# A two-layer spectral kernel: operand forms in the Newton square roots, and column groups in the forward DFT over w

## The chip, the cores and the metric

The kernel runs on one core of a Trainium2 chip. The metric is the device time in microseconds of one execution, and for several executions their median.

## The reference

The input x is a float32 array of 32 images, 32 channels, 128 rows (h) and 128 columns (w). There are two layers, and each adds its result to its input.

The first layer normalises x over groups of two channels and then takes a matrix square root of every 128x128 channel by five steps of a coupled Newton iteration (1024 matrices in all):

```
Y = A / |A|;  Z = I
for 5 steps:  T = 0.5 * (3 I - Z Y);  Y = Y T;  Z = T Z
x = x + Y * sqrt(|A|)
```

The second layer normalises again, takes the real part of a two-dimensional Fourier transform, and keeps 64 of 128 row frequencies (the first 32 and the last 32) and the first 32 column frequencies. For every kept frequency it multiplies the 32 channels by a 32x32 matrix of weights, takes the inverse transform, and adds its real part:

```
X = fftn(gn(x), axes=(2, 3)).real
top = einsum('bixy,ioxy->boxy', X[:, :, :32, :32], weights1)
bot = einsum('bixy,ioxy->boxy', X[:, :, -32:, :32], weights2)
x = x + ifftn(zero-padded(top, bot)).real
```

## The kernel before

Everything is float32. The work has three phases. The first goes over the images: normalisation, the square roots, and the forward transform of each image to the kept frequencies, which stay in SBUF in the tile `xs` (partition, row frequency within a group of 16, column frequency, image). The second multiplies by the weights and transposes the result into `ot`. The third takes the inverse transform for each image, adds it to the first layer's output, which the first phase left in HBM (`mid`), and writes the result.

In the first phase, `prep` loads an image into `xt` (h on partitions) in four transfers on SP's queue and works out the statistics, mostly on VectorE. `newton` handles four channels at once, a "group" of four 128x128 matrices in one [128, 512] tile. Every product of two such tiles is four TensorE matmuls into one PSUM bank (`products`), and every transpose four TensorE transposes against an identity (`transposed`). A bank is taken out of PSUM by ScalarE as a plain copy (`taken`) or by VectorE as 1.5 I - 0.5 ps (`three_less`). GpSimd (POOL) writes the normalised group. Five PSUM banks serve these products, two the forward transform (`ps_ax`), one the statistics.

The first product of the iteration is with the identity, so that it needs none. With P standing for the matrix that would turn A into Y, the kernel before keeps `p` and the transpose of A, `at`, and multiplies

```
            for _ in range(NSTEPS - 2):
                ty = taken(products(p, at), "ty", 5)
                yield
                tt = three_less(products(p, ty), "tt", 5)
                yield
                p = taken(products(tt, p), "p", 6)
                yield
```

TensorE computes the transpose of its first operand times the second, so in this form every product comes out as the next one needs it, and the only transpose in a group is that of A.

`post` sends the finished image to `mid`, takes its statistics, and then, for each four channels, normalises (`xn`, on POOL), and transforms over h with the data as stationary operand and 128 columns of the table moving (64 frequencies, cosine and sine; line 271). ScalarE copies the result into `u`, with channels innermost. Then comes the transform over w (line 281): for each of 16 row indices, two accumulating matmuls with a 128x128 block of `u` stationary and 32 columns of the table moving. The bank that results has frequency rows and channels on partitions, and VectorE copies it to `xs` (line 290).

The order of the first phase is set by hand: four lanes each run one group's generator, started three rounds apart, each advancing by one `yield` per round; after each round one step of `prep` or `post` (the list `back`) is taken. The tile framework then places the instructions on the engines' queues, keeping dependencies. [...]

Of the kernel before, what the change touches and what calls it, by code (L numbers as in the profile page):

```python
# [19 lines left out]
F32 = mybir.dt.float32  # L20
# [6 lines left out]
P = 128  # L27
B = 32
C = 32
# [3 lines left out]
EPS = 1e-5  # L33
KIN = 16
L = 32


T_FH = slice(0, 128)
T_FW = slice(128, 192)
T_IW = slice(192, 448)  # L40
T_IH = slice(448, 576)
T_COLS = 576


@with_exitstack
def conv_preact_kernel(
# [31 lines left out]
    with ExitStack() as phase:  # L78
# [90 lines left out]
        def bank(pool, tag):  # L169
            return pool.tile([P, 4, P], F32, tag=tag, name=tag)  # L170
# [26 lines left out]
        def newton(g, xt, nm, sc, sn):  # L197

            chans = range(4 * g, 4 * g + 4)
            a = nsp.tile([P, 4, P], F32, tag="a", name="a", bufs=4)
            for j, c in enumerate(chans):
                nc.gpsimd.tensor_scalar(  # L204
                    a[:, j, :],
                    xt[:, c, :],
                    nm[:, c // 2 : c // 2 + 1],
                    sc[:, c : c + 1],
                    ALU.add,
                    ALU.mult,  # L210
                )
            yield
            p = three_less(a, "p", 6)
            at = taken(transposed(a), "at", 5)
            yield
            for _ in range(NSTEPS - 2):
                ty = taken(products(p, at), "ty", 5)
                yield
                tt = three_less(products(p, ty), "tt", 5)
                yield  # L220
                p = taken(products(tt, p), "p", 6)
                yield
            ty = taken(products(p, at), "ty", 5)
            yield
            t = three_less(products(ty, p), "tt", 5)
            yield
            ps = products(ty, t)
            for j, c in enumerate(chans):
                nc.vector.scalar_tensor_tensor(  # L229
                    xt[:, c, :], ps[:, j, :], sn[:, c : c + 1], xt[:, c, :], ALU.mult, ALU.add  # L230
                )
            yield

        def post(b, xt):

            nc.sync.dma_start(out=mid[b], in_=xt)
            st = small.tile([P, C, 6], F32, tag="b_st", name=f"b_st{b}")
            for c in range(C):
                nc.vector.bn_stats(st[:, c, :], xt[:, c, :])
                if c % 8 == 7:  # L240
                    yield
            nm, pq = stats(st, "b")
            yield
            vg = small.tile([P, G], F32, tag="b_vg", name=f"b_vg{b}")
            nc.vector.tensor_reduce(
                vg, pq.rearrange("p (g c) -> p g c", c=2), AX.X, ALU.add
            )
            v = small.tile([P, G], F32, tag="b_v", name=f"b_v{b}")
            nc.vector.tensor_scalar(v, vg, 0.5, EPS, ALU.mult, ALU.add)
            s = root(v, G, "b_r", 256.0)  # L250
            r = small.tile([P, G], F32, tag="b_inv", name=f"b_inv{b}")
            nc.vector.reciprocal(r, s)  # L252
            yield

            u = up.tile([P, P, C], F32, tag="u", name=f"u{b}")
            for q in range(C // 4):
                xn = nsp.tile([P, 4, P], F32, tag="xn", name=f"xn{b}_{q}", bufs=2)
                for i in range(2):
                    g = 2 * q + i
                    nc.gpsimd.tensor_scalar(  # L260
                        xn[:, 2 * i : 2 * i + 2, :],
                        xt[:, 2 * g : 2 * g + 2, :],
                        nm[:, g : g + 1],
                        r[:, g : g + 1],
                        ALU.add,
                        ALU.mult,
                    )
                yield
                ps = bank(ps_ax, "ax")
                for j in range(4):  # L270
                    nc.tensor.matmul(  # L271
                        ps[:, j, :], xn[:, j, :], tab[:, T_FH], start=True, stop=True
                    )
                nc.scalar.copy(u[:, :, 4 * q : 4 * q + 4], ps.rearrange("w c m -> w m c"))
            yield

            uv = u.rearrange("w (s k r) c -> w s k (r c)", s=2, r=4)
            ps = ps_ax.tile([P, KIN, L], F32, tag="ax", name=f"f{b}")
            for kin in range(KIN):
                for s in range(2):  # L280
                    nc.tensor.matmul(  # L281
                        ps[:, kin, :],
                        uv[:, s, kin, :],
                        tab[:, T_FW.start + s * L : T_FW.start + (s + 1) * L],
                        start=(s == 0),
                        stop=(s == 1),
                    )
                if kin % 4 == 3:
                    yield
            nc.vector.tensor_copy(xs[:, :, :, b], ps)  # L290
            yield

        made = {}
# [32 lines left out]
    with ExitStack() as phase:  # L326
        wp = phase.enter_context(tc.tile_pool(name="wp", bufs=2))
        mp = phase.enter_context(tc.tile_pool(name="mp", bufs=2))
        ps_m = phase.enter_context(tc.tile_pool(name="ps_m", bufs=1, space=PSUM))
        ps_t = phase.enter_context(tc.tile_pool(name="ps_t", bufs=3, space=PSUM))  # L330
        for kq in range(4):
            wt = wp.tile([P, C, 4, L], F32, tag="wt", name=f"wt{kq}")
            for r in range(4):
                src = (w1, w2)[r // 2]
                k0 = (r % 2) * KIN + 4 * kq
                nc.sync.dma_start(
                    out=wt[32 * r : 32 * r + 32], in_=src[:, :, k0 : k0 + 4, :]
                )

            om = mp.tile([P, 4, 8, 4, L], F32, tag="om", name=f"om{kq}")  # L340
            for lh in range(2):

                pm = [
                    ps_m.tile([P, 16, C], F32, tag=f"pm{r}", name=f"pm{kq}_{lh}_{r}")
                    for r in range(4)
                ]
                for k4 in range(4):
                    for l in range(16):
                        for r in range(4):
                            nc.tensor.matmul(  # L350
                                pm[r][32 * k4 : 32 * k4 + 32, l, :],
                                xs[32 * r : 32 * r + 32, 4 * kq + k4, 16 * lh + l, :],
                                wt[32 * r : 32 * r + 32, :, k4, 16 * lh + l],
                                start=True,
                                stop=True,
                            )
                for r in range(4):
                    src = pm[r].rearrange("p l (o4 og) -> p og o4 l", o4=4)
                    dst = om[:, r, :, :, 16 * lh : 16 * lh + 16]
                    if r % 2:  # L360
                        nc.vector.tensor_copy(dst, src)  # L361
                    else:
                        nc.scalar.copy(dst, src)
            for r in range(4):
                omr = om[:, r].rearrange("p og o4 l -> p og (o4 l)")
                for h in range(2):
                    pt = ps_t.tile([P, 4, 4, B], F32, tag="pt", name=f"pt{kq}_{r}_{h}")
                    for i in range(4):
                        nc.tensor.transpose(pt[:, i].rearrange("p k b -> p (k b)"), omr[:, 4 * h + i, :], ident)  # L369
                    k0 = KIN * r + 4 * kq  # L370
                    dst = ot[:, 4 * h : 4 * h + 4, k0 : k0 + 4, :]
                    if h:
                        nc.vector.tensor_copy(dst, pt)
                    else:
                        nc.scalar.copy(dst, pt)
# [41 lines left out]
def _table():  # L417

    import numpy as np

    k = np.concatenate([np.arange(32), np.arange(96, 128)])
    n = np.arange(P)
    row = 2 * np.pi * (np.outer(n, k) % P) / P
    col = 2 * np.pi * (np.outer(n, np.arange(L)) % P) / P
    t = np.zeros((P, T_COLS))
    rows = np.stack([np.cos(row), np.sin(row)]).reshape(2, P, 4, KIN)
    t[:, T_FH] = rows.transpose(1, 0, 3, 2).reshape(P, P)
    t[:, T_IH] = rows.transpose(0, 2, 3, 1).reshape(P, P)
    t[:, T_FW] = np.concatenate([np.cos(col), -np.sin(col)], 1)
    t[:, T_IW] = np.tile(np.concatenate([np.cos(col).T, -np.sin(col).T], 1) / (P * P), (4, 1))  # L430
    return t.astype(np.float32)

# [22 lines left out]
```

## Time and profile before

| | |
|---|---|
| Time, median of 3 runs | 4153.58 us (4152.88 to 4153.66) |
| Profiled execution | time 4153.58 us, span 4151.8 us |
| TensorE matmul / weight load busy | 3973.8 us (96%) / 3781.8 us (91%) |
| VectorE, ScalarE, POOL busy | 1983.4 us (48%), 1498.5 us (36%), 730.4 us (18%) |
| First phase | to about 3400 us |
| Granted TensorE clock | 1.00 in most of the first phase, mean 0.954 |

Busy time is the union of an engine's instructions, and TensorE's matmuls and weight loads stand in rows of their own (PE and PEld), since a load can lie beside a matmul. A float32 product appears as two pairs of load and matmul, a transpose as one. A row of the page gives line, engine, operation, output and input tiles, shapes and count, then the busy time in us and the mean of one in ns, then the idle time of the engine just ahead of it with what ended it. The means of matmuls contain the way through the array, so that what a stream of them costs is read from the distance between starts.

### The profile page before, as it was taken

To read this page: it belongs to the slowest core of one execution; us is meant where nothing else is said; L and a number is where in the kernel's file an instruction comes from. 1 tells how busy PE (TensorE), PEld (TensorE's weight loads), DVE (VectorE), ACT (ScalarE), POOL (GpSimd) and SP (SyncE) were. 2 spreads that over 40 slices of the span, in tenths; PEclk is the share of its full clock that TensorE was granted. 3 is DMA by queue.
4 is the path that set the end of the run, shared out by engine and by line. 5 is a ranking of instruction groups with operands and counts; after the bars stand their busy time and mean duration, and the time that the engine had idled before them with its cause. 6 is when DMAs were issued, how large, how long until landed. Compare 5 with 4: busy or idle time off the path is not lost.

```text
span 4151.8 us, 90922 instructions
## 1 busy us (share of the span) xinstructions
PE 3973.8 (96%) x38784; PEld 3781.8 (91%) x38784; DVE 1983.4 (48%) x5766; ACT 1498.5 (36%) x2689; POOL 730.4 (18%) x1542
## 2 busy tenths in 40 slices
PE   7999999999999999999999999999999989987777
PEld 7999999999999999999999999999999988853333
DVE  5555555555555555555555555555555420023333
ACT  3444444444434444343344444334344320022222
POOL 2222222222222222222222222222222100000000
PEclk9999999999999999999999999999999975578998
DMA  2111111111111111111111111111111021168887
GB/s 65 42 42 42 42 42 42 42 42 42 42 42 42 42 42 42 42 42 42 42 42 42 42 41 39 37 40 40 40 39 38 21 62 22 22 203 280 285 285 247
DMA packets 291620, 282.95 MB, mean 68 GB/s; under 512 B 4368, under 2 KB 282896, under 8 KB 283024
## 3 DMA queue, kind: packets, MB, share of 16 engines
q1 hardware_dynamic: 159120, 210.02, 15.8%
q10 hardware_dynamic: 132096, 67.11, 5.5%
q8 instruction: 306, 5.01, 0.5%
q14 instruction: 98, 0.80, 0.1%
HBM read 142.90 MB, written 134.22 MB: 67 GB/s over the span
## 4 chain that ended last, share of the span: by engine, by line
PE 92%; DMA 2%; ACTq 2%; DVE 2%; ACT 1%; issue 0%; SPq 0%; POOL 0%; POOLq 0%; DVEq 0%
PE ns L186 65%; PE py L407 7%; PE pm L350 5%; PE ax L271 5%; PE f L281 5%; PE ns L194 3%; ACTq L411 2%; DMA xt<-in_x 2%; PE pg L396 1%; ACT gt L405 1%; PE pt L369 1%; DVE yt L409 1%; DVE a_st L136 0%; SPq L129 0%; DVE om L361 0%
## 5 line engine op out<-in xcount | busy, mean ns | idle before, releaser
L175 DVE SCALAR_TENSOR_TENSOR tt<-ns,eye 128x512 f32<-128x512 f32 x1024 | 704.8, 688 | 1111.3 <-PE ns L186 1104.8
L186 PE MATMUL ns<-at,p 128*128 128x128 f32 x8192 | 981.3, 276 | 1.4 <-DVE a_st L136 0.7
L186 PEld LDWEIGHTS ns<-at,p 128*128 128x128 f32 x8192 | 944.8, 192 | 2.1 <-ACT p L180 1.1
L180 ACT COPY p<-ns 128x512 f32<-128x512 f32 x768 | 449.7, 586 | 1062.2 <-PE ns L186 1058.1
L204 POOL TENSOR_SCALAR a<-xt,a_nm,a_sc 128x128 f32<-128x128 f32 x1024 | 444.3, 448 | 1789.0 <-PE ns L194 1423.2
L186 PE MATMUL ns<-p,tt 128*128 128x128 f32 x6144 | 754.5, 276 | 4.4 <-DVE tt L175 4.2
L186 PE MATMUL ns<-ty,p 128*128 128x128 f32 x6144 | 752.4, 276 | 0.4 <-ACT ty L180 0.4
L180 ACT COPY ty<-ns 128x512 f32<-128x512 f32 x1024 | 599.8, 586 | 403.2 <-PE ns L186 403.2
L186 PEld LDWEIGHTS ns<-p,tt 128*128 128x128 f32 x6144 | 719.4, 193 | 5.6 <-DVE tt L175 5.5
L186 PEld LDWEIGHTS ns<-ty,p 128*128 128x128 f32 x6144 | 717.8, 192 | 0.5 <-ACT ty L180 0.5
L260 POOL TENSOR_SCALAR xn<-xt,b_nm,b_inv 128x256 f32<-128x256 f32 x512 | 286.0, 569 | 865.8 <-DVE b_inv L252 467.0
L229 DVE SCALAR_TENSOR_TENSOR xt<-ns,a_t_s,xt 128x128 f32<-128x128 f32 x1024 | 288.4, 344 | 224.2 <-PE ns L186 224.2
L407 PE MATMUL py<-gt,tab 128*128 128x512 f32 x512 | 273.5, 683 | 115.2 <-ACT gt L405 112.6
L407 PEld LDWEIGHTS py<-gt,tab 128*128 128x128 f32 x512 | 105.8, 218 | 241.7 <-ACT gt L405 147.5
L409 DVE TENSOR_TENSOR yt<-py,yt 128x512 f32<-128x512 f32 x256 | 176.6, 692 | 297.9 <-PE py L407 289.4
L186 PE MATMUL ns<-p,ty 128*128 128x128 f32 x2048 | 280.5, 278 | 0.7 <-ACT ty L180 0.7
L271 PE MATMUL ax<-tab,xn 128*128 128x128 f32 x2048 | 272.1, 277 | 2.7 <-POOL xn L260 2.7
L186 PE MATMUL ns<-tt,ty 128*128 128x128 f32 x2048 | 273.2, 276 | 0.8 <-DVE tt L175 0.8
L405 ACT COPY gt<-pg 128x512 f32<-128x512 f32 x256 | 131.4, 599 | 341.1 <-issue 176.6
L271 PEld LDWEIGHTS ax<-tab,xn 128*128 128x128 f32 x2048 | 251.0, 193 | 3.2 <-POOL xn L260 3.0
L186 PEld LDWEIGHTS ns<-p,ty 128*128 128x128 f32 x2048 | 251.6, 192 | 0.9 <-ACT ty L180 0.9
L136 DVE BATCH_NORM_STATS2 a_st<-xt 128x6 f32<-128x128 f32 x1024 | 217.8, 279 | 68.0 <-DMA xt<-in_x 66.6
(75 smaller groups left out, 2795.8 us busy)
## 6 DMA issues: line engine op xcount, KB each, us to landing
xt<-in_x SPq DMA_DIRECT2D x128, 512.0 KB, 6.8
mid<-xt SPq DMA_DIRECT2D x32, 2048.0 KB, 6.3
yt<-mid SPq DMA_DIRECT2D x32, 2048.0 KB, 8.6
out<-yt ACTq DMA_DIRECT2D x64, 1024.0 KB, 8.0
wt<-in_L_conv_weights SPq DMA_DIRECT2D x16, 512.0 KB, 9.2
tab<-in_table SPq DMA_DIRECT2D x1, 288.0 KB, 3.0
```

What stands on the lines that cost most here:

```text
L136: nc.vector.bn_stats(st[:, c, :], xt[:, c, :])
L175: nc.vector.scalar_tensor_tensor(t, ps, -0.5, eye15, ALU.mult, ALU.add)
L180: nc.scalar.copy(t, ps)
L186: nc.tensor.matmul(ps[:, j, :], lhsT[:, j, :], rhs[:, j, :], start=True, stop=True)
L204: nc.gpsimd.tensor_scalar(a[:, j, :], xt[:, c, :], nm[:, c // 2 : c // 2 + 1], sc[:, c : c + 1], ALU.add, ALU.mult,)
L229: nc.vector.scalar_tensor_tensor(xt[:, c, :], ps[:, j, :], sn[:, c : c + 1], xt[:, c, :], ALU.mult, ALU.add)
L260: nc.gpsimd.tensor_scalar(xn[:, 2 * i : 2 * i + 2, :], xt[:, 2 * g : 2 * g + 2, :], nm[:, g : g + 1], r[:, g : g + 1], ALU.add, ALU.mult,)
L271: nc.tensor.matmul(ps[:, j, :], xn[:, j, :], tab[:, T_FH], start=True, stop=True)
L281: nc.tensor.matmul(ps[:, kin, :], uv[:, s, kin, :], tab[:, T_FW.start + s * L : T_FW.start + (s + 1) * L], start=(s == 0), stop=(s == 1),)
L350: nc.tensor.matmul(pm[r][32 * k4 : 32 * k4 + 32, l, :], xs[32 * r : 32 * r + 32, 4 * kq + k4, 16 * lh + l, :], wt[32 * r : 32 * r + 32, :, ...
L407: nc.tensor.matmul(py, tab[:, T_IH], gt, start=True, stop=True)
L409: nc.vector.tensor_add(xt[:, o : o + 4, :], py, xt[:, o : o + 4, :])
```

## The change

The change has two parts.

In `newton`, the iteration keeps `y` (Y) and `zt` (the transpose of Z). Each of the three inner steps computes T = 1.5 I - 0.5 Z Y, transposes T on TensorE, and multiplies for the new Y and the new Z's transpose. The first step has one product, the last two. The POOL output and Y share the tile tag `y` with eight buffers.

In `post`, the transform over h gives only the 65 columns that are different: 33 cosines (`KC`) and 32 sines (`KS`); cosines and sines of negative frequencies are the same up to a sign. The transform over w then has the table as stationary operand, 32 columns at a time, and `u` moving, up to 512 columns. Each of four frequency groups `r4` writes its own 32 PSUM partitions, so each occupies one 32-column group of TensorE, and two matmuls (cosine and sine) accumulate in each. The bank that results has column frequencies on partitions, and VectorE transposes it in 32x32 blocks on its way to `xs`, in place of the copy. The negative frequencies come in descending order, so the table for the inverse transform and the order of the weights' rows follow suit.

```diff
-T_FH = slice(0, 128)
-T_FW = slice(128, 192)
-T_IW = slice(192, 448)
-T_IH = slice(448, 576)
-T_COLS = 576
+KC = 33
+KS = 32
+T_FH = slice(0, KC + KS)
+T_FW = slice(65, 161)
+T_IW = slice(161, 417)
+T_IH = slice(417, 545)
+T_COLS = 545
...
             chans = range(4 * g, 4 * g + 4)
-            a = nsp.tile([P, 4, P], F32, tag="a", name="a", bufs=4)
+            y = nsp.tile([P, 4, P], F32, tag="y", name="y0")
             for j, c in enumerate(chans):
                 nc.gpsimd.tensor_scalar(
-                    a[:, j, :],
+                    y[:, j, :],
...
             yield
-            p = three_less(a, "p", 6)
-            at = taken(transposed(a), "at", 5)
+
+            zt = three_less(transposed(y), "zt", 8)
+            yield
+            y = taken(products(zt, y), "y", 8)
             yield
             for _ in range(NSTEPS - 2):
-                ty = taken(products(p, at), "ty", 5)
+                t = three_less(products(zt, y), "t", 5)
                 yield
-                tt = three_less(products(p, ty), "tt", 5)
+                tt = taken(transposed(t), "tt", 5)
                 yield
-                p = taken(products(tt, p), "p", 6)
+                py, pz = products(tt, y), products(t, zt)
+                y, zt = taken(py, "y", 8), taken(pz, "zt", 8)
                 yield
-            ty = taken(products(p, at), "ty", 5)
-            yield
-            t = three_less(products(ty, p), "tt", 5)
-            yield
-            ps = products(ty, t)
+            tt = three_less(products(y, zt), "tt", 5)
+            yield
+            ps = products(tt, y)
...
-            u = up.tile([P, P, C], F32, tag="u", name=f"u{b}")
+            u = up.tile([P, KC + KS, C], F32, tag="u", name=f"u{b}")
...
-                ps = bank(ps_ax, "ax")
+                ps = ps_ax.tile([P, 4, KC + KS], F32, tag="ax", name=f"h{b}_{q}")
...
-            uv = u.rearrange("w (s k r) c -> w s k (r c)", s=2, r=4)
-            ps = ps_ax.tile([P, KIN, L], F32, tag="ax", name=f"f{b}")
-            for kin in range(KIN):
-                for s in range(2):
+            ps = ps_ax.tile([P, KIN, C], F32, tag="ax", name=f"f{b}")
+            for s in range(2):
+                for r4 in range(4):
+                    first = (0, 16, 17, 1)[r4]
+                    skip = int(s == 1 and first == 0)
+                    at = first + skip if s == 0 else KC + first + skip - 1
+                    cols = T_FW.start + L * (0 if s == 0 else 1 + r4 // 2)
                     nc.tensor.matmul(
-                        ps[:, kin, :],
-                        uv[:, s, kin, :],
-                        tab[:, T_FW.start + s * L : T_FW.start + (s + 1) * L],
+                        ps[32 * r4 : 32 * r4 + 32, skip:, :],
+                        tab[:, cols : cols + L],
+                        u[:, at : at + KIN - skip, :],
                         start=(s == 0),
                         stop=(s == 1),
                     )
-                if kin % 4 == 3:
-                    yield
-            nc.vector.tensor_copy(xs[:, :, :, b], ps)
+            yield
+
+            nc.vector.transpose(xs[:, :, :, b], ps)
             yield
...
-                k0 = (r % 2) * KIN + 4 * kq
+                k0 = (4 * kq, KIN + 4 * kq, 12 - 4 * kq, 28 - 4 * kq)[r]
...
-                                wt[32 * r : 32 * r + 32, :, k4, 16 * lh + l],
+                                wt[32 * r : 32 * r + 32, :, (k4, 3 - k4)[r // 2], 16 * lh + l],
```

The host's table function follows: cosines and sines of 0 to 32 and 1 to 32 for the transform over h, the three blocks cosine, -sine, sine for w, and the rows of the inverse transform in the new order.

More of the change, by code (lines that the diff above doesn't have):

```diff
@@ L419, in _table @@
     import numpy as np
-    k = np.concatenate([np.arange(32), np.arange(96, 128)])
+    kin = np.arange(KIN)
+    k = np.concatenate([kin, KIN + kin, -(17 + kin), -(1 + kin)])
     n = np.arange(P)
-    row = 2 * np.pi * (np.outer(n, k) % P) / P
+    row = 2 * np.pi * (np.outer(k, n) % P) / P
+    mag = 2 * np.pi * (np.outer(n, np.arange(KC)) % P) / P
     col = 2 * np.pi * (np.outer(n, np.arange(L)) % P) / P
     t = np.zeros((P, T_COLS))
[L426 to L429, printed above, removed]
+    t[:, T_FH] = np.concatenate([np.cos(mag), np.sin(mag[:, 1:])], 1)
+    t[:, T_IH] = np.concatenate([np.cos(row), np.sin(row)])
+    t[:, T_FW] = np.concatenate([np.cos(col), -np.sin(col), np.sin(col)], 1)
     t[:, T_IW] = np.tile(np.concatenate([np.cos(col).T, -np.sin(col).T], 1) / (P * P), (4, 1))
```

## The prediction

> **What bounds the kernel now.** I read the page's busy shares first, then the busy time by stage, then the chain of work that ended last, and then TensorE's two rows in order of time.
>
> ```profile
> PE 3973.8 (96%) x38784; PEld 3781.8 (91%) x38784; DVE 1983.4 (48%) x5766; ACT 1498.5 (36%) x2689; POOL 730.4 (18%) x1542
> ```
>
> The table of three windows inside the first phase (columns: window; length; busy us and instructions of each engine; granted clock; DMA) says that this is no average over unlike stages: TensorE has no gap for 3 ms.
>
> ```profile
> 200.00:1200.00 1000.00, 998.59 (x8928) 998.26 (x8927) 534.42 (x1633) 400.36 (x714) 212.18 (x448) 1.00 0.13 41
> 1200.00:2200.00 1000.00, 998.65 (x8943) 998.32 (x8942) 531.30 (x1631) 401.00 (x715) 221.12 (x464) 1.00 0.13 41
> 2200.00:3200.00 1000.00, 998.90 (x8944) 998.57 (x8944) 533.27 (x1635) 403.74 (x721) 217.06 (x459) 1.00 0.13 41
> ```
>
> Some 8,930 matmuls in 1000 us are one each 112 ns, and so many weight loads. VectorE works 53% and ScalarE 40% of it. The chain of work repeats once per image; two of its longest pieces give the period, 1044.08 - 939.58 = 104.5 us.
>
> ```profile
> 939.58 9.01 PE ns L186 x80
> 1044.08 9.01 PE ns L186 x80
> ```
>
> An image issues, from the page's counts over 32: products 24576/32 = 768, transposes 1024/32 = 32, the DFT over h (L271) 64, the DFT over w (L281) 64, statistics 8: 936 pairs of load and matmul. 104.5 us / 936 = 111.6 ns. So the phase is a count of pairs, whatever their kind. The weight loads in order of time (start us, length us, then the instructions) show it for each kind:
>
> ```profile
> 2070.08 2.76 PEld L186 LDWEIGHTS ns<-ty,p 128*128 128x128 f32 x24
> 2072.76 1.87 PEld L281 LDWEIGHTS f<-tab,u 128*128 128x128 f32 x16
> ...
> 2077.81 0.47 PEld L194 LDWEIGHTS ns<-ident,a 128*128 128x128 f32 x4
> 2078.25 1.87 PEld L281 LDWEIGHTS f<-tab,u 128*128 128x128 f32 x16
> 2080.04 3.65 PEld L186 LDWEIGHTS ns<-at,p 128*128 128x128 f32 x32
> ```
>
> From start to start: products (2072.76 - 2070.08) / 24 = 112 ns; DFT over w, 32 moving columns, (2080.04 - 2078.25) / 16 = 112 ns; transposes (2078.25 - 2077.81) / 4 = 110 ns. A pair that moves 32 columns costs as much as one that moves 128: with 128x128 stationary, the load sets the pace. An f32 product is two such pairs (the page counts 8192 for 4 x 1024 products), a transpose one.
>
> **What the Trainium skill says.** "TensorE: Matmul & The Clock Gate", section "LDWEIGHTS (loading the stationary operand)", gives a load P/1.2 ns for P columns: 107 ns for 128. The trace agrees within 5% (111.6). The same page, "Part 3: Packing small matmuls — row/col tiling", says that matmuls on distinct 32-row or 32-column tiles run beside each other (2.38x for three column tiles). The trace has such a stage, the inverse DFT (32x64 tiles, four row and two column groups):
>
> ```profile
> 3707.52 0.19 PEld L407 LDWEIGHTS py<-gt,tab 128*128 128x128 f32 x1 [0.36 <-issue]
> 3707.95 0.19 PEld L407 LDWEIGHTS py<-gt,tab 128*128 128x128 f32 x1 [0.24 <-issue]
> 3708.38 0.19 PEld L407 LDWEIGHTS py<-gt,tab 128*128 128x128 f32 x1 [0.24 <-issue]
> ...
> 3709.33 1.40 PE L396 MATMUL pg<-tab,ot 32*64 32x128 f32 x64
> ```
>
> The first three lines, 0.43 us apart, price a pair of 512 moving columns at full array; 128 columns are a quarter, 0.107. The last line has 64 pairs of 128 columns in 1.40 us, not 64 x 0.107 = 6.9: 4.9 beside each other, more than four row groups alone give. "TensorEngine Tiling (Array Packing)", "Key Properties", says that changing the tiling mode drains TensorE; no line here isolates that.
>
> **The change, part by part** (against the profiled execution: span 4151.8, time 4153.58, which is also the median of the runs).
>
> *Square roots, products.* Before, a group of four channels takes 3 x 3 + 3 = 12 products and 1 transpose. After: 1 + 3 x (1 + 2) + 2 = 12 products and 1 + 3 = 4 transposes. Products add nothing. Three transposes of four channels in 256 groups are 3072 pairs; at the 0.110 us of above **+338 us**, all on the path, since TensorE has no gap to take them.
>
> *Square roots, evacuation.* ScalarE copies 8 banks a group before, 10 after: 512 x 0.586 = +300 us, less some 54 for the shorter copies of the DFT over h (below): from 40% to some 45% of the phase, hidden beside TensorE. VectorE keeps 5 banks a group (the first now from PSUM, 0.69 instead of 0.68). 0 us.
>
> *New waits.* A loop step is now t (VectorE), its transpose (ScalarE), then two products needing it. Lanes start three rounds apart and a group takes 15 rounds as before, so the four lanes stand at the same kind of step together: a round of transposes is 4 x 0.44 = 1.8 us of TensorE, where every round had up to 4 x 0.89 = 3.6. The last lane's transpose needs its t: VectorE 0.69 plus the 0.2 gap that the trace shows ahead of such reads; three transposes cover 1.3 us of it. The next round's first product needs ScalarE's 0.59 + 0.25, covered by 1.3. What gets in between is VectorE's other work ahead of t in its queue (four statistics, 0.86 us; four output adds, 1.13 us), and behind a blocked transpose stand all lanes. Bounds: 0, and 0.3 us in each of 256 x 15 / 4 / 3 = 320 such rounds, 96. Below nothing is excluded: there was no wait to remove. I take **+15**. PSUM stays at five banks for the products; each is held some 1.8 us of a group's 12.
>
> *POOL.* It writes y where it wrote a. a had four buffers of its own; y shares eight, five allocations a group. The buffer eight back is free at least one product round (5 us) earlier than needed, against 1.8 us of writing: 0, inside the bounds above.
>
> *DFT over h.* 65 moving columns for 128, same 2048 pairs with 128x128 stationary. By the L281 pace (32 columns, 112 ns) this saves **0**; bounds 0 and 8 us (down to 107). Its copy on ScalarE shrinks from 512 to 260 elements (at most half of 0.586 less; I take 0.21); hidden.
>
> *DFT over w.* Goes: 64 pairs an image, 7.14 us. Comes: 8 matmuls with 32 stationary columns and 512 (once 480) moving, 16 pairs, four column groups. Beside each other, each group does 4 pairs of 0.43 = 1.7 us; with the drain on both sides I take 2.1 (bounds 1.7 and 16 x 0.43 = 6.9, nothing overlapping). That is -5.0 x 31 = -156. The last image runs alone, 11.39 us at a granted clock of 0.62; after, some 3.8: -7.6. Together **-164**; bounds -176 and -8.
>
> *Block transpose.* VectorE's 32 copies at 1.053 us become transposes. "VectorE: DVE Perf Modes", "The three transpose paths", says it does 32x32 blocks only, which is what is wanted here; 311 ns for 128x128 bf16, by it an estimate of 4 x 311 = 1.2 us for 512 columns. Bounds 0.7 (a contiguous eviction) and 2.1; only the last image's stands on the path: 0 within 1 us. post has three steps fewer, so its tail is no longer.
>
> *The rest.* Weight loads from HBM keep count and size, each on SP as before; the mixing matmuls and inverse transforms only read other addresses; the table is 6% smaller. 0. Starting and draining four lanes with longer steps: +3.
>
> Sum: 338 + 15 - 164 + 3 = +192: 4153.6 + 192 = **4346 us**.
>
> **Rivals.**
>
> *Column groups do not run beside each other* (the change does not do what it says in its main part). The stationary is all 128 rows high here, and two column groups, never four, are seen sharing the array. Then the w-DFT is 6.9 us against 7.14: 338 + 15 + 3 - 8 = +348, 4502. Half overlap, each tile's second pass holding back the next tile, is 9 of 16 slots, 3.9 us: -100 instead of -164, 4410. Against: 4.9 beside each other in the inverse DFT.
>
> *The short round exposes latency.* 0.3 us in each of the 320 rounds: 4346 + 81 = 4427. For: all lanes are in step. Against: VectorE is half idle, and the trace shows statistics matmuls placed between a lane's products, so that TensorE's order leaves room to fill.
>
> *Faster: short matmuls are not paced by their weight load.* If a pair with few moving columns cost its stream (54 ns for a transpose's 128 columns in one pass, 55 for 65 columns in h), the transposes would add 166, the h-DFT would save 116 and the w-DFT 164: -114, 4040. It decides where the pace c meets 3072 c - 2048 (111.6 - c) = 164 us, c = 77 ns; below that the change is faster. Against it stand the L281 and L194 lines, both at 110 to 112.
>
> **How the numbers follow.** The likeliest case, four groups beside each other and few stalls, has 0.68, on its own 4310 to 4390; the exposed latency 0.14; half overlap 0.08, none 0.06; the fast case 0.02; the rest a lower granted clock (the page "TensorE: Matmul & The Clock Gate", "Part 4: PE-mode transpose", says that transposes do not count as activity; here the clock reads 1.00 through bursts of 0.44 us, and bursts become 1.8). The range 4295 to 4470 leaves out no overlap, the fast case and the tails, under 2 in 10. A difference of 0.2%, 8 us, is about what a measurement of this kernel can tell from no change; nearly all cases lie far above it: slower 0.97, same 0.01, faster 0.02.
>
> **What would show it.** Transposes 4096 on TensorE, still 110 ns apart; h-DFT pairs still 112 apart; the w-DFT some 2 us from first to last of 16; the image period near 110 us; TensorE still over 98% busy in the phase with waits for VectorE's t and ScalarE's tt of tens of us at most; ScalarE near 45% there; the stages after the first phase unchanged. Wrong would be: a period over 113, matmuls of a w-DFT starting 0.43 us apart, or transposes under 77 ns.

## The result and the profile after

| | before | after |
|---|---|---|
| Time, median of 4 | 4153.23 us (4150.50 to 4153.66) | 4348.14 us (4342.37 to 4352.01) |
| Profiled execution: time, span | 4153.58, 4151.8 us | 4352.01, 4350.2 us |
| First phase, to the first mixing matmul | 3399.7 us | 3591.3 us |
| Mixing phase | 268.8 us | 273.3 us |
| Inverse transforms | 483.3 us | 485.6 us |

The changed kernel is slower by 195 us: ratio 1.047, 95% interval 1.0451 to 1.0488. The forecast was 4346. In the profiled executions 191.6 us of it lie in the first phase. The 4.5 us in the mixing phase appear in some profiles of the changed kernel and not in others (269.4 in one of the experiments below), and nothing here explains them.

The busy times of the page of the changed kernel:

```profile
PE 4166.8 (96%) x40320; PEld 3900.9 (90%) x40320; DVE 1975.7 (45%) x5766; ACT 1726.6 (40%) x3201; POOL 720.3 (17%) x1542
```

TensorE has 40320 - 38784 = 1536 pairs more: 3072 transposes came, 1536 pairs of the DFT over w went. The count alone would be 1536 x 0.112 = 172 us.

The same three windows as before (length; busy us and instructions of PE, PEld, DVE, ACT, POOL; granted clock; DMA):

```profile
200.00:1200.00 1000.00, 997.92 (x8887) 977.52 (x8886) 501.42 (x1551) 445.11 (x823) 202.34 (x432) 1.00 0.12 40
1200.00:2200.00 1000.00, 999.09 (x8900) 977.75 (x8899) 503.84 (x1559) 443.51 (x821) 202.35 (x432) 1.00 0.12 40
2200.00:3200.00 1000.00, 999.05 (x8903) 979.20 (x8900) 503.10 (x1551) 445.66 (x825) 202.34 (x432) 1.00 0.12 39
```

TensorE's matmuls still fill the phase and ScalarE stands at 44 to 45%, as forecast. What differs is the weight-load row, 978 where it was 998: it now has gaps. From the groups by line and shape of the changed kernel (busy us, mean ns; idle ahead and its causes):

```profile
L196 PEld LDWEIGHTS ns<-ident,t 128*128 128x128 f32 x3072 | 346.1, 142 | 42.2 <-DVE t L177 18.6 <-DVE a_st L138 17.6 <-issue 0.8
L274 PE MATMUL h<-tab,xn 128*128 128x65 f32 x2048 | 262.9, 273 | 2.7 <-POOL xn L263 2.7
L277 ACT COPY u<-h 128x260 f32<-128x260 f32 x256 | 96.3, 376 | 296.2 <-PE h L274 296.2
L288 PEld LDWEIGHTS f<-u,tab 128*32 128x32 f32 x512 | 13.6, 110 | 24.2 <-issue 19.9 <-ACT u L277 0.7
L297 DVE STREAM_TRANSPOSE xs<-f 128x512 f32<-128x512 f32 x32 | 34.1, 1066 | 24.9 <-PE f L288 24.9
```

Some of these gaps belong to the new DFT over w: its 32-column loads are short (110 ns in the mean, against 192 for a product's), and the array streams meanwhile. Others are waits: the loads of the loop's transposes wait 36 us, for t or for statistics that stand ahead of t in VectorE's queue. The block transpose takes 1.066 us for the copy's 1.053.

TensorE in order of time around one DFT over w (start, length, instructions) shows both:

```profile
2083.75 1.00 PE L274 MATMUL h<-tab,xn 128*128 128x65 f32 x8
2084.59 2.90 PE L188 MATMUL ns<-y,zt 128*128 128x128 f32 x24
2087.42 1.92 PE L288 MATMUL f<-u,tab 128*32 128x512 f32 x16
2089.28 2.21 PE L196 MATMUL ns<-ident,t 128*128 128x128 f32 x12
2091.33 0.60 PE L196 MATMUL ns<-ident,y 128*128 128x128 f32 x4
...
2198.38 1.93 PE L288 MATMUL f<-u,tab 128*32 128x512 f32 x16
```

The 16 pairs of the DFT over w last 2089.28 - 2087.42 = 1.86 us; one after another at 0.43 they would need 6.9. The next comes after 110.96 us (the mean of 28 such periods in the trace is 110.6, against 104.5 in the part of the kernel before that the prediction showed). The round of transposes after it is the telling place: the 12 pairs of three lanes' t take 2.05 us where the last 4 take 0.43, the pace of 0.11. What holds them stands in the timeline of all engines for these microseconds:

```profile
2086.23 1.65 DVE L138 BATCH_NORM_STATS2 a_st<-xt 128x6 f32<-128x128 f32 x8 [0.88 <-DMA xt<-in_x]
2087.42 0.16 PEld L288 LDWEIGHTS f<-u,tab 128*32 128x32 f32 x8
...
2087.88 0.13 PEld L288 LDWEIGHTS f<-u,tab 128*32 128x32 f32 x4 [0.30 <-issue]
2088.30 0.13 PEld L288 LDWEIGHTS f<-u,tab 128*32 128x32 f32 x4 [0.30 <-issue]
2088.32 0.29 DVE L138 BATCH_NORM_STATS2 a_st<-xt 128x6 f32<-128x128 f32 x1 [0.44 <-DMA xt<-in_x]
2088.53 0.67 DVE L177 SCALAR_TENSOR_TENSOR t<-ns,eye 128x512 f32<-128x512 f32 x1
2089.12 0.28 DVE L138 BATCH_NORM_STATS2 a_st<-xt 128x6 f32<-128x128 f32 x1
2089.27 0.42 PEld L196 LDWEIGHTS ns<-ident,t 128*128 128x128 f32 x4 [0.84 <-DVE t L177]
...
2089.32 0.67 DVE L177 SCALAR_TENSOR_TENSOR t<-ns,eye 128x512 f32<-128x512 f32 x1
2089.91 0.28 DVE L138 BATCH_NORM_STATS2 a_st<-xt 128x6 f32<-128x128 f32 x1
2090.04 0.42 PEld L196 LDWEIGHTS ns<-ident,t 128*128 128x128 f32 x4 [0.35 <-DVE t L177]
```

VectorE works through the next image's statistics, waits for their load from HBM on the way, and only then makes t. TensorE's loads of transposes each wait for one t of 0.67 us. After the first 60 us, every wait of more than a few nanoseconds of these loads stands in this round, within 6 us of the start of the image's DFT over w; the other rounds of transposes run without one.

The lines also show the column groups at work: their loads come in sets of four, one for each group (the first two sets together), and each further set about 0.42 us after the last.

### The profile page after: what moved, and what is told of

Its sections match the earlier page's. It is cut to its first block, busy times and chain, and to the rows that moved or that the text cites. A ratio compares the mean times of both kernels' runs of the same rounds, so it can differ in the third digit from the quotient of the medians.

```text
span 4350.2 us, 94753 instructions
## 1 busy us (share of the span) xinstructions
PE 4166.8 (96%) x40320; PEld 3900.9 (90%) x40320; DVE 1975.7 (45%) x5766; ACT 1726.6 (40%) x3201; POOL 720.3 (17%) x1542
## 5 line engine op out<-in xcount | busy, mean ns | idle before, releaser
L188 PE MATMUL ns<-y,tt 128*128 128x128 f32 x8192 | 1087.7, 276 | 1.8 <-ACT tt L182 1.0
L188 PE MATMUL ns<-y,zt 128*128 128x128 f32 x8192 | 1024.9, 276 | 1.2 <-DVE zt L177 0.8
L188 PEld LDWEIGHTS ns<-y,tt 128*128 128x128 f32 x8192 | 994.6, 192 | 6.1 <-ACT tt L182 1.7
L188 PEld LDWEIGHTS ns<-y,zt 128*128 128x128 f32 x8192 | 965.0, 192 | 2.5 <-DVE zt L177 1.1
L177 DVE SCALAR_TENSOR_TENSOR t<-ns,eye 128x512 f32<-128x512 f32 x768 | 529.3, 689 | 663.1 <-PE ns L188 650.5
L188 PE MATMUL ns<-zt,t 128*128 128x128 f32 x6144 | 819.2, 275 | 0.0
L182 ACT COPY y<-ns 128x512 f32<-128x512 f32 x1024 | 600.4, 586 | 412.4 <-PE ns L188 412.4
L188 PEld LDWEIGHTS ns<-zt,t 128*128 128x128 f32 x6144 | 750.6, 192 | 0.0
L182 ACT COPY zt<-ns 128x512 f32<-128x512 f32 x768 | 450.2, 586 | 240.1 <-PE ns L188 240.1
L177 DVE SCALAR_TENSOR_TENSOR tt<-ns,eye 128x512 f32<-128x512 f32 x256 | 177.1, 692 | 701.5 <-PE ns L188 701.5
L196 PEld LDWEIGHTS ns<-ident,t 128*128 128x128 f32 x3072 | 346.1, 142 | 42.2 <-DVE t L177 18.6
```

Source lines behind the costliest of these rows:

```text
L177: nc.vector.scalar_tensor_tensor(t, ps, -0.5, eye15, ALU.mult, ALU.add)
L182: nc.scalar.copy(t, ps)
L188: nc.tensor.matmul(ps[:, j, :], lhsT[:, j, :], rhs[:, j, :], start=True, stop=True)
L196: nc.tensor.transpose(ps[:, j, :], t[:, j, :], ident)
```

## The experiments

Theory A, that of the prediction: the added transposes cost their pace on TensorE, column groups run beside each other, and a small rest is waits in the rounds of transposes. The rivals put the cost into the longer chain through VectorE and ScalarE, or deny the overlap of the column groups. The kernel before was run beside each set of experiments, and its median lay between 4152.92 and 4156.49 us; differences below some 5 us between kernels of different sets say nothing. Where starts of TensorE are added up below, each matmul counts with the distance from its start to the next one's start.

### Each part by itself

Only `newton` of the change (`post`, the tables and the mixing as before):

> Only the new form of the square roots, with the forward DFT of the kernel before. Theory A (the change costs its 3072 added transposes on TensorE, 0.110 us each, plus some 15 to 40 us of short waits): 4153 + 338 + 15 to 40 = 4506 to 4531 us. Theory B (TensorE has slack for the transposes, and the added time of the whole change comes from elsewhere): 4153 to 4250. If the two parts of the change add up, this run minus the changed kernel is what the new DFT gives, 160 to 180.

Measured: 4561.94 us (4555.51 to 4568.11), ratio 1.0977 (1.0958 to 1.0995), +405 us. That is above theory A's range by 31 us, and theory B is out.

Only the forward DFT of the change (`post`, the tables and the mixing as changed, `newton` as before):

> Only the new forward DFT (65 columns over h, column groups over w, block transpose), with the square roots of the kernel before. Theory A: four column groups run beside each other, so 64 pairs of 0.112 us become 1.9 us per image, with 0 to 13 us from the narrower DFT over h: 4153 - 164 to -185 = 3968 to 3989. If column groups gave only half overlap: 4050. If none: 4145. A change that does not interact: its difference to before plus that of the square roots alone makes the 195 us of both.

Measured: 3987.72 us (3985.91 to 3988.81), ratio 0.9594 (0.9579 to 0.9608), -169 us, inside the range of full overlap. This version beats both kernels.

The parts alone add up to 405 - 169 = 237 us; together they cost 195. So 42 us of the square roots alone are a matter of the company they keep. The trace of that kernel shows two things: its waits for t, 32 us, and a clock that falls. First its row in the view of waits (us in total, times, longest), then two windows of it (the granted clock is the third number from the end) and TensorE just before and in the first of them:

```profile
PEld ns L194 <- DVE t L175: 32.0, 64, 1.3
```

```profile
1026.00:1036.60 10.60, 10.60 (x54) 10.60 (x55) 1.12 (x4) 2.44 (x5) 0.00 (x0) 0.54 0.01 2
1036.66:1046.90 10.24, 10.24 (x94) 10.24 (x94) 2.81 (x5) 2.49 (x5) 1.75 (x4) 1.00 0.00 0
```

```profile
1018.70 2.84 PE L186 MATMUL ns<-y,zt 128*128 128x128 f32 x24
1021.38 1.87 PE L282 MATMUL f<-tab,u 128*128 128x32 f32 x16
1024.18 1.45 PE L194 MATMUL ns<-ident,t 128*128 128x128 f32 x8 [0.92 <-DVE t L175]
1025.95 1.12 PE L194 MATMUL ns<-ident,t 128*128 128x128 f32 x4 [0.33 <-DVE t L175]
1026.86 1.06 PE L194 MATMUL ns<-ident,y 128*128 128x128 f32 x4
1027.71 3.46 PE L282 MATMUL f<-tab,u 128*128 128x32 f32 x16
```

Full products run until 1021.4. Then come four microseconds of matmuls with 32 columns, a wait and transposes, and from 1025.5 on the same kinds of work run at half pace: 54 instructions in a stretch that otherwise holds 94. The trace has seven such stretches inside the phase, 58 us in all; half of that, some 29 us, is lost. The page "TensorE: Matmul & The Clock Gate" of the Trainium skill, "Part 4: PE-mode transpose", says that transposes do not count as activity for the clock. The falls here fit that, but do not isolate it. The kernel before has one such stretch too (713.9 us, 3.4 long), behind 32-column matmuls and a wait of 0.58 us, with no transpose in the six microseconds ahead; a kernel further below has one (1987.4 us, 3.4 long) behind transposes and a wait of 1.22 us, with no matmul of 32 moving columns. What all nine share is a DFT over w followed by a wait of TensorE of 0.3 to 1.2 us, within 5 us ahead of the fall. Other waits as long were followed by none (0.87 us at 2910.7 in this trace), so what it takes stays open.

The same kernel with its lanes four rounds apart:

```diff
-                if lanes[i] is None and todo and rounds >= 3 * i:
+                if lanes[i] is None and todo and rounds >= 4 * i:
```

> The new square roots with the forward DFT of before, lanes started four rounds apart. That form with lanes three apart took 4562, 68 more than 4156 + 338; its trace has 58 us at half clock inside the first phase and VectorE waits ahead of transposes. If both come from rounds in which four transposes stand together next to matmuls with 32 moving columns: 4494 to 4510, and no half clock in the phase. If the clock falls whatever the order of the lanes: above 4520.

Measured: 4482.04 us (4479.24 to 4484.86), +329 us, 12 below the range. The clock reads 1.00 in all three windows of its phase and the waits for t are 2 us. So both the half clock and the waits hang on the lanes standing at the same kind of step; since they go together, this run cannot say whether the clock fell for the transposes or for the waits. The two make some 59 of the 76 us that the other order of the lanes saves. Without them the square roots cost 329 / 3072 = 0.107 us a transpose. In the trace the transposes themselves start 111.7 ns apart, which is 343 us for the added ones; the other pairs start a little closer than in the kernel before (products 112.6 ns for 113.0, the DFT over w 108.7 for 112.0), which gives some 15 us back. Why is not known.

### Transposes or their chain

```diff
-                tt = taken(transposed(t), "tt", 5)
+                tt = taken(t, "tt", 5)
```

> The changed kernel without the transpose in the three inner steps: ScalarE copies t from SBUF where it copied the transposed t from PSUM, so the result is another matrix, while the order t, copy, two products and all waits on VectorE and ScalarE stay. 2304 groups' worth of nothing else changes; 3072 TensorE transposes go. Theory A (TensorE time): 4348 - 336 = 4012, less 10 to 30 if the short rounds of transposes exposed waits, 3982 to 4012. Theory B (the longer chain through VectorE and ScalarE costs the time): over 4250, since the chain is kept.

(The figure 2304 in that text is a slip; 3072 transposes go.) Measured: 4008.68 us (4005.45 to 4013.77), 339.5 us below the changed kernel, with the chain kept. So nearly all of the cost is TensorE's time for the transposes, and theory B is out.

The chain is not quite free, though. This kernel has exactly as many pairs as the one with the forward DFT alone (37248 on both pages), and is 21 us slower than its 3987.72. Its waits show where:

```profile
PEld ns L188 <- DVE tt L177: 19.7, 33, 1.0
```

The round of transposes has shrunk to the one of y, and the product behind it waits for VectorE's tt: the starts from a transpose to the next instruction take 133.9 us in the phase here, 114.2 with the forward DFT alone, for 1024 transposes each. So this run took some waits away with the transposes and put others in their place, and its 339.5 is the price of the transposes only because the two are about equal.

### The lanes' phases

The same edit, four rounds for three, in the changed kernel:

> The changed kernel with the lanes started four rounds apart in place of three, so that they no longer stand at the same kind of step together (15 rounds a group, steps repeat every 3). Theory A with waits in the short rounds: the rounds of four transposes go, and 15 to 30 us with them, 4318 to 4333. Theory C (the extra beyond the transposes is not due to the lanes being in step): within 5 us of the changed kernel's 4348.

Measured: 4327.30 us (4323.50 to 4329.05), 20.8 us below the changed kernel; its first phase ends at 3569.5 us, 21.8 earlier. The wait of the loop's transposes for t, in the view of waits (us in total, times, longest):

```profile
PEld ns L196 <- DVE t L177: 2.0, 3, 1.1
```

That row had 18.6 in the changed kernel, beside 17.6 for the statistics, which is gone. Of these 34 us, only 21 became time, since a load that waits while the array still streams the DFT over w delays nothing (shown under the next heading but one). So some 21 us of the change come from the lanes standing in step, most of it waits in the rounds of transposes: the starts from a transpose to the next instruction fall from 468.2 to 455.9 us, and those of the statistics' matmuls from 38.4 to 34.2.

### The column groups

The first group's sums done four times:

```diff
-            for s in range(2):
-                for r4 in range(4):
+            for s, r4 in [(s, 0) for _ in range(3) for s in range(2)] + [
+                (s, r4) for s in range(2) for r4 in range(4)
+            ]:
+                if True:
```

> The changed kernel, where the first column group works its own sums of the DFT over w four times over (three times ahead, overwritten by the last), the other three groups once: 28 pairs per image in place of 16, 12 of the added ones in one column group. Theory A (each column group streams at its own 0.43 us per 512 columns, beside the others): the first group's 16 pairs take 6.9 us where the stage took 1.86, so 5.0 us more per image, 4348 + 160 = 4508. Rival (no groups beside each other, a pair with few stationary columns just streams faster, 1.86 / 16 = 0.116 us each): 12 x 0.116 = 1.4 us more per image, 4393.

Measured: 4492.85 us (4491.76 to 4493.37), +144.7 us against the changed kernel, 4.5 an image, near the 5.0 of groups with a stream each and far from 1.4. TensorE in order of time:

```profile
2048.45 6.84 PE L290 MATMUL f<-u,tab 128*32 128x512 f32 x28
2055.22 1.53 PE L196 MATMUL ns<-ident,t 128*128 128x128 f32 x12
2056.59 0.60 PE L196 MATMUL ns<-ident,y 128*128 128x128 f32 x4
```

28 pairs take 6.77 us, just 16 x 0.42: the one long group, with the other three beside it. And the 12 pairs after it take 1.37 us where they took 2.05: the longer stage gives VectorE the time to make t. Over the phase the stage takes 155.5 us more, 4.9 an image, and the transposes 9.0 less, 0.3 an image. That is most of what the sum falls short of 5.0.

The loops exchanged, so that each group's matmuls are issued together:

```diff
-            for s in range(2):
-                for r4 in range(4):
+            for r4 in range(4):
+                for s in range(2):
```

> The changed kernel with the loops of the DFT over w exchanged: each column group's cosine and sine matmuls follow each other, and then comes the next group. Same 16 pairs. If TensorE lets a later column group start while an earlier one still has pairs waiting: 1.9 us per image as now, within 10 us of 4348. If a pair that waits for its own group holds up all behind it: 4 + 3 + 3 + 3 = 13 times 0.43 = 5.6 us, 3.7 more per image, 4348 + 118 = 4466.

Measured: 4351.44 us (4349.57 to 4357.49). No difference, and the stage takes 2088.10 - 2086.23 = 1.87 us:

```profile
2086.23 1.94 PE L288 MATMUL f<-u,tab 128*32 128x512 f32 x16
2088.10 1.77 PE L196 MATMUL ns<-ident,t 128*128 128x128 f32 x12
```

A later group starts while pairs of an earlier one still wait for their own columns.

### The width of the DFT over h

```diff
-                ps = ps_ax.tile([P, 4, KC + KS], F32, tag="ax", name=f"h{b}_{q}")
+                ps = ps_ax.tile([P, 4, P], F32, tag="ax", name=f"h{b}_{q}")
...
-                        ps[:, j, :], xn[:, j, :], tab[:, T_FH], start=True, stop=True
+                        ps[:, j, :], xn[:, j, :], tab[:, 0:P], start=True, stop=True
...
-                nc.scalar.copy(u[:, :, 4 * q : 4 * q + 4], ps.rearrange("w c m -> w m c"))
+                nc.scalar.copy(u[:, :, 4 * q : 4 * q + 4], ps[:, :, 0 : KC + KS].rearrange("w c m -> w m c"))
```

> The changed kernel with 128 moving columns in the DFT over h again (the 63 added columns are other parts of the table and their results are not used); copies and all else unchanged. Theory A (the weight load of 128 columns sets the pace): within 4 us of the changed kernel. Theory B (starts read 0.105 us apart with 65 columns in the changed kernel's trace, against 0.112: a real gain of 0.05 us per bank): 256 x 0.05 = 13 us slower, 4361.

Measured: 4373.03 us (4370.78 to 4377.77), 25 us slower: outside both theories. TensorE's pace is not the reason. The changed kernel, 65 columns:

```profile
2054.43 1.00 PE L274 MATMUL h<-tab,xn 128*128 128x65 f32 x8
2055.27 1.11 PE L188 MATMUL ns<-y,zt 128*128 128x128 f32 x8
2056.21 1.06 PE L188 MATMUL ns<-y,tt 128*128 128x128 f32 x8
```

This kernel, 128 columns:

```profile
2068.86 1.06 PE L274 MATMUL h<-tab,xn 128*128 128x128 f32 x8
2069.76 1.06 PE L188 MATMUL ns<-y,zt 128*128 128x128 f32 x8
2070.65 1.06 PE L188 MATMUL ns<-y,tt 128*128 128x128 f32 x8
```

With 65 columns the bank's eight pairs take 0.84 us to the next start and the following product 0.94; with 128 they take 0.90 and 0.89. Both sums are 1.78 or 1.79: the narrower matmul starts the product sooner and the product takes it back. It is so over the whole phase: the starts of the DFT over h take 222.9 us with 65 columns and 232.3 with 128, those of the products 2782.8 and 2773.4, and the two together 3005.7 in both kernels. What differs is the starts after the transposes and after the DFT over w, 13.6 and 8.6 us longer with 128 columns: waiting, by the view of waits of this kernel.

```profile
PEld ns L196 <- DVE t L177: 50.6, 71, 2.2
PEld ns L196 <- DVE a_st L138: 8.4, 10, 0.8
```

59 us for the 36 of the changed kernel. The instructions' order in the two kernels differs at this point: the framework put 29 of the next image's statistics ahead of the first t in VectorE's queue, where the changed kernel has 25 (both read from one image each). I took the late load of that image for the reason and gave it a fourth buffer, in both widths and in the kernel with the DFT alone:

```diff
-        xp = phase.enter_context(tc.tile_pool(name="xp", bufs=3))
+        xp = phase.enter_context(tc.tile_pool(name="xp", bufs=4))
```

> The changed kernel with four image buffers in place of three, so that the next image's load can start earlier. In the changed kernel the statistics of the next image stand ahead of t in VectorE's queue and wait for the load (84 us in all), and TensorE's transposes wait behind them, 36 us. If the late load is what makes the waits: 4348 less 15 to 30, 4318 to 4333. If it is the number of statistics in the queue and not their wait for the load: within 5 us of 4348.

Measured: 4347.70 us (4341.25 to 4351.73), no difference. In the profiled executions the waits for the load fell from 84 to 62 us and those of the transposes from 36 to 26, but these two executions are the slowest of the changed kernel's and the fastest of this one's, 11 us apart, while the medians agree.

> The changed kernel with 128 moving columns in the DFT over h and four image buffers. With three buffers the 128 columns cost 25 us, and VectorE's queue had 29 of the next image's statistics ahead of the first t in place of 25. If that cost is waits for the load in front of t: within 5 us of the kernel with 65 columns and four buffers. If it is the columns themselves: 13 to 25 us above that kernel.

Measured: 4365.47 us (4362.43 to 4373.03), 18 above the same kernel with 65 columns. The cost of the width stays, so the late load is not what makes it. The number lies where "the columns themselves" would put it, but the starts say otherwise again: the DFT over h and the products together take 3006.3 us in both kernels, and the starts after transposes 15.9 us more with 128 columns. So the cost is waiting for t. That the longer queue ahead of t makes the waiting is argued from the order and the waits: no kernel with the same order and the other width was run.

> The new forward DFT with the square roots of before and four image buffers. If the waits for VectorE's tt there come from the late load as well: 3965 to 3980, else 3988 within 5.

Measured: 3991.96 us (3991.12 to 3993.51): no gain.

> The new forward DFT with the square roots of before, lanes four rounds apart. With three apart it took 3988, and its trace has some 20 us in which TensorE waits for VectorE's tt after the short DFT over w. If those come from the lanes standing at the same kind of step: 3965 to 3980. If not: 3988 within 5.

Measured: 4007.91 us (4005.94 to 4012.20), 20 us slower than with lanes three apart. Both forecasts of a gain failed for one reason, in how I read the waits. The row of the kernel with the DFT alone was

```profile
PEld ns L188 <- DVE tt L177: 20.9, 25, 1.0
```

These waits come right after the DFT over w, while the array still streams its 512 columns. With the lanes four apart the load there waits for no tt, and yet the next product starts 0.52 us after the last matmul of the DFT over w in both kernels (the mean of 30 images). So a weight load that waits there delays nothing. Why the lanes four apart cost that kernel 20 us was not settled; 12 us of it lie in the starts of the products. The edit that helps one form of the square roots hurts the other, so the 21 us that it gained in the changed kernel may be net of such a loss.

## Why the prediction was right

**Bound.** The phase is a count of pairs. Over the whole phase a pair takes 113.0 ns in the kernel before and 112.4 with the square roots alone and lanes four apart, for the 111.6 of the prediction.

**Transposes, +338.** Taking them away gave 339.5, adding them alone without the waits 329. The term was right to 3%.

**DFT over w, -164.** 1.86 us for 2.1 assumed; the last image's is 3.19 for 3.8. The DFT alone gave -169. The rival of no overlap fell with the first group's quadruple work, that of half overlap with the 1.86 us and with the exchanged loops, which cost nothing.

**DFT over h, 0.** The size was right: what the narrower matmul saves, the products take back. The forecast that its pairs would still start 112 ns apart was wrong (0.84 us for eight, 105 ns). And the width is not free in the other direction: 128 columns would have cost 18 to 25 us more by way of waits for t. The prediction had no such term.

**Waits, +15.** Measured by the lanes' phases: 21, perhaps net. The place was the one forecast, a round of transposes with VectorE's statistics ahead of t, but the forecast had four statistics there and the trace has 25, which also wait for their load. The rival of 81 us had the same place and overrated it: it put a wait into each of 320 rounds, and the trace has them in one round per image. The late load alone does not make them (four image buffers gained nothing), nor does the shortened DFT over w, since the square roots alone, with the long DFT, have 32 us of waits for t.

**Evacuation, POOL, block transpose, 0.** ScalarE rose to 44 to 45% and its copy of `u` is 0.376 us. The view of waits has TensorE waiting some 2 us for ScalarE's tt in the phase. The block transpose is 1.066 us against the estimate of 1.2.

**The faster rival** (short matmuls not paced by their load) is out: transposes keep 0.107 to 0.112 us. Its sum was also wrong by the prediction's own lines. It took 54 ns for the 128 columns of a transpose, but at 0.43 us for a pair of 512 columns they stream in 107 ns, and with that the rival comes to about +50 us instead of -114. So a transpose could not have told the load from the stream; the matmuls with 32 columns could, and did, at 112 ns.

**Sum.** The term of 338 measured 329 to 339.5, that of -164 measured -169, that of 15 measured 21, and the 3 for start and end was not measured. The measured terms add up to between 181 and 192, for the 195 of the runs. That the forecast came within 2 us of the median is luck: errors of some 5 us, in the DFT over w and in the waits, cancelled.

The chance of 0.02 for a lower clock did not come true in the changed kernel, whose clock is 1.00 up to the last images of the phase. In the square roots alone the clock did fall, and cost about 29 us; by what mechanism is open. Had the square roots been changed alone, the terms 338 + 15 + 3 would have missed the measured 405 by 49 us.

## What to carry to other kernels

When TensorE has no gap, count its pairs of load and matmul: an operand order that saves VectorE or ScalarE nothing and adds a transpose is paid in full, while a narrow operand belongs on the stationary side, one column group for each independent piece. Judge the two halves of a change apart; here one gained 4% and the other lost more. An engine that is busy half the time (VectorE here) can still hold up the bound one, where its queue puts a row of other work ahead of one short result. And before a wait in a trace is counted as time, look whether the next start moves without it: 21 us of waits in the kernel with the DFT alone were worth nothing.

## What the runs showed of the hardware that I had not expected

The granted clock can halve while TensorE is never idle for more than 1.3 us: seven stretches of 3 to 10 us in the square roots alone, each behind 32-column matmuls, a short wait and transposes, and none once the lanes were spread out. One stretch in the kernel before had no transposes ahead of it, and one in a kernel with four image buffers (and 128 columns over h) no matmuls with 32 moving columns, so neither is needed by itself. Column groups need no interleaved order: four groups of four pairs took 1.9 us in either order. And fewer moving columns than the weight load covers (65 for 128) bring forward the next start by 0.05 us without making the stream of pairs any shorter: 3005.7 us for the DFT over h and the products together, in both widths.
